# Loading the weights of Q, K and V with 32 instead of 4 rows outermost, in a two-layer graph attention kernel

## The chip, the cores and the metric

The kernel runs on one core of a Trainium2 chip. A core has five engines that run their own instruction queues in order and meet only at semaphores: TensorE (PE: matmuls, with weight loads as a second stream, PEld), VectorE (DVE), ScalarE (ACT), GpSimd (POOL) and SyncE (SP), which here only issues transfers. Sixteen DMA engines move data between HBM (the chip's memory) and SBUF (the core's working memory); TensorE writes its sums to PSUM. The metric is device time in microseconds (us), the median of several runs. All data are 32-bit floats.

## The reference

The input is a batch of 128 graphs of 128 nodes with 512 features, and one 128 x 128 adjacency matrix for each graph. Two layers follow each other, each with a residual and a layer norm:

```python
# layer 0
q, k, v = x @ Wq + bq, x @ Wk + bk, x @ Wv + bv        # 8 heads of 64
attn = softmax(where(adj > 0, q @ k.T / sqrt(64), -1e9))
x = layernorm(x + relu((attn @ v) @ Wo + bo))
# layer 1
Wh = x @ W
e = leaky_relu((Wh @ a1)[:, None] + (Wh @ a2)[None, :], 0.2)
x = layernorm(x + elu(softmax(where(adj == 0, -1e9, e)) @ Wh))
```

## The kernel before

The kernel works through 64 pairs of graphs. The five large products (Q, K, V, O and W) of a pair are done as block products in the manner of Strassen and Winograd: seven products (`PRODUCTS`) with sums of blocks on both sides, gathered in three PSUM banks A, B and C. The sums of the weight blocks are made once at the start (`weight_sums`, L131 to L134): for Q and K together they need both blocks of Wq and both of Wk. The sums on the left side (`left_sums`, L151 to L154, tiles sx, so, sz) are made for each pair, on GpSimd. VectorE and ScalarE empty the banks between the products (u2, u3, kT, qT, e1a, e1b and so on); a product that writes a bank again must wait for that.

Layer 1 doesn't multiply Wh by a1 and a2: `fold_a` (L203 to L213) multiplies W by a at the start (tiles wa_scr, wa_rep), `fold_t` and `fold_out` spread the result over the partitions (pwa, wa_bc), and `edge_term` (L490) then takes one product and sum for each graph. Each half of a is loaded by a transfer (a_bc) that GpSimd issues.

The attention weights are transposed in two steps: 32 x 32 blocks on VectorE (`weights_t`, prb), then out to HBM and back with the blocks reordered (`weights_out`, prd; `weights_in`, prT), from which `mix_values` (po) reads them. In layer 1 the row terms (pj), the edge matrix (pat) and the mixed nodes (pz) pass through TensorE.

The order of all this is not written as a loop. `at` gives every step of every pair a due time, PLAN[step] plus the pair's number times PERIOD, and the steps are recorded in the order of the due times. So PLAN sets only the order in which instructions stand in each engine's queue; their waits set the times. BUFS says how many buffers each kind of tile has: with one, a new tile waits until the last reader of the one before is done.

Ahead of the pairs come the loads of the weights, in this order: the first x blocks (xb), Wq, Wk, the adjacency matrix (adj), the second x blocks and adjacency matrix, then Wv, Wo and W. Wq and Wv are issued from ScalarE's queue, all else from SyncE's. Each load has one of eight completion semaphores and waits until the transfer that had it before is done. The rows of x are reordered in blocks of 32 (partition 32 v + r holds feature 128 v + r of a chunk), so Wq, Wk and Wv are loaded by `load_block_x` with the same order; Wo and W come row by row (`load_block`, L120).

The first work on VectorE waits for bq (bqs, L194), then scales both blocks of Wq (L196), transposes the first x blocks (L288) and makes the sums.

Of the kernel before, what the change touches and what calls it, by code (L numbers as in the profile page):

```python
# [14 lines left out]
N_BATCH = 128  # L15


PERIOD = 80.36
PLAN = dict(
    load_blocks=-203.35, load_adj=-141.65, x_transpose0=-108.79, x_transpose1=-80.72, sums_qk=-62.62, mask=-35.32,  # L20
    sums_v=-33.81, x_sums=-30.87, qk0=-30.03, qk_p1=-28.89, qk1=-24.47, qk_p1q=-23.84, qk_p6=-23.67, qk4=-22.15,
    qk3=-21.47, qk2=-20.46, qk_p7=-19.06, qk_c11=-17.42, qk_c22=-16.69, qk5=-15.77, v0=-13.29, sums_fold0=-12.95,
    v_p1=-11.35, fill_logits1=-10.97, qk6=-9.66, qk_c21=-9.52, v1=-8.33, v2=-7.72, v_p6=-6.99, v3=-6.55,
    fill_logits0=-4.19, qk_c12=-2.81, sums_o=-1.37, logits0=0.0, v_p7=1.78, mask_logits0=6.87, logits1=6.98,
    v4=8.58, v_c11=11.52, max_logits0=11.75, mask_logits1=12.17, v_c22=12.53, v5=17.32, max_logits1=17.42,
    v_c21=18.18, v6=18.57, v_c12=18.66, exp_logits0=26.37, sum_logits0=28.64, exp_logits1=31.22, norm_logits0=33.91,
    fill_edges0=36.7, sums_fold1=37.99, sums_fold_t0=42.14, sum_logits1=47.8, load_x0=56.09, norm_logits1=56.91,
    weights_t0=57.44, sums_fold_out0=60.06, weights_out0=61.6, weights_in0=62.47, sums_fold_t1=65.58,
    weights_t1=67.46, sums_fold_out1=74.55, mix_values0=81.46, weights_out1=82.7, weights_in1=84.68,
    mix_values1=87.22, mix_values_out0=94.58, mix_values_out1=96.97, sums_w=98.84, o_sums=103.62, o0=108.53,  # L30
    load_x1=109.41, o_p1=114.18, fill_edges1=114.73, o1=117.76, o_p1l=118.1, o2=120.61, o_p6=122.66, o3=122.75,
    o_p7=123.47, o4=123.68, o_c11=126.83, o_c22=129.32, o5=129.79, o_c21=130.83, residual01=132.36, o6=132.67,
    o_c12=133.46, stats01=133.46, mean01=133.56, residual00=134.07, rstd01=136.55, stats00=137.12, shift01=137.46,
    mean00=137.78, norm01=137.87, rstd00=137.95, edge_term01=138.68, edge_term11=139.19, shift00=140.27,
    norm00=141.75, edge_term10=142.12, edge_term00=142.31, edge_row1=143.18, edge_sums1=143.88, edge_row0=145.26,
    edge_leaky1=147.3, edge_sums0=147.37, edge_mask1=149.05, edge_leaky0=150.02, edge_max1=150.22,
    edge_mask0=151.47, edge_max0=152.05, edge_exp1=152.16, edge_exp0=152.23, edge_norm1=152.34, edges_t1=152.35,
    edges_t0=154.18, edges_t_out1=154.18, edge_norm0=154.29, mix_nodes1=154.39, edges_t_out0=154.42,
    mix_nodes0=154.6, mix_nodes_out1=156.09, mix_nodes_out0=157.89, z_sums=164.73, w0=173.41, w1=179.87,
    w_p1=181.52, w_p6=182.07, w2=182.1, w3=185.01, w_p7=187.54, w4=187.83, w_c11=188.88, w_c22=190.51, w5=195.11,  # L40
    w6=195.64, w_c21=198.1, elu_exp1=198.84, w_c12=200.38, elu_low1=215.59, elu_max1=222.2, elu_exp0=222.5,
    elu_low0=228.48, residual11=235.55, elu_max0=240.61, stats11=243.8, mean11=247.72, rstd11=249.46,
    residual10=251.29, shift11=265.27, stats10=269.96, mean10=297.04, finish1=299.37, rstd10=315.64, store1=320.24,
    shift10=323.36, finish0=332.2, store0=341.53)

ENDS = {}

BUFS = dict(
    xb=2, adj=4, xT=3, sx=2, pr=2, e1a512=1, e1b512=1, mask=1, u2512=1, u3512=2, qT=2, kT=2, e1a256=2, cv=2,
    u2256=1, u3256=1, t=2, scr=2, cw=4, prb=1, prT=2, oT=2, x=2, at=3, so=1, e1b256=2, co=5, e=2, attT=7, zT=2,  # L50
    sz=1)


# [1 line left out]
def tile_two_graph_layers(ctx: ExitStack, tc: tile.TileContext, x, adj, wq, bq, wk, bk, wv, bv, wo, bo, w, a, out,  # L55
# [9 lines left out]
    P = 128  # L65
    D = x.shape[2]
# [54 lines left out]

    def load_block_x(t, k, queue, src, rows, cols):

        for c in range(2):
            queue.dma_start(t[:, k, c, :], bass.AP(
                tensor=src.tensor, offset=src.offset + 32 * (2 * rows + c) * D + cols.start,
                ap=[[P * D, 4], [D, 32], [1, cols.stop - cols.start]]))

    def weight_sums(t, eng):
        b11, b21, b22, t1, t2, t3, t4 = (t[:, k, :, :] for k in range(7))  # L130
# [38 lines left out]
    wqk = block_weight("wqk", D)  # L169
    load_blocks(0)  # L170
    load_block_x(wqk, 0, nc.scalar, wq, 0, everything)
    load_block_x(wqk, 1, nc.scalar, wq, 1, everything)
    load_block_x(wqk, 5, nc.sync, wk, 0, everything)
    load_block_x(wqk, 2, nc.sync, wk, 1, everything)
    load_adj(0)
# [400 lines left out]
    def at(key, p, fn, *args):  # L576

        shift = ENDS.get(p if p < n_pair // 2 else p - n_pair, {}).get(key, 0.0)
        events.append((p * PERIOD + PLAN[key] + shift, len(events), fn, args))

# [69 lines left out]
```

## Time and profile before

Three runs took 2509.44, 2513.02 and 2514.66 us (median 2513.02). The profiled run had a span of 2509.6 us.

| Engine | busy us | share of the span |
|---|---|---|
| TensorE, matmuls | 2413.6 | 96% |
| TensorE, weight loads | 2190.1 | 87% |
| VectorE | 1912.0 | 76% |
| ScalarE | 1607.5 | 64% |
| GpSimd | 1459.9 | 58% |

The shares are means over the span. The matmuls of one pair follow each other in about 37.4 us, 64 pairs long, with a start and an end in which fewer steps overlap. The chain of work that ended last is 83% TensorE and 7% transfers. In the profile's lines, "L257" is the line of the kernel, "pBqk<-sx,wqk" the tile written and those read, "x16" the number of instructions in a row. Lines of waits give total time, number and the longest wait.

The loads of the weights in the profile are 4 transfers of 256 KB for Wq, 4 for Wk, and 8 of 128 KB for Wv, Wo and W each.

### The profile page before, as it was taken

The numbers are of one execution on the slowest core, as the hardware profiler recorded it, in microseconds if no ns is written. First come the engines' busy times: TensorE is split into PE (matmuls) and PEld (weight loads), VectorE is DVE, ScalarE is ACT, GpSimd is POOL, SyncE is SP. The second block draws the span as 40 slices with busy tenths as digits, with TensorE's granted clock in tenths as the row PEclk, the third lists the DMA queues.
The fourth block names the chain that finished last, engine by engine and source line by source line (L and its number), as shares of the span: only waits on it lengthen the run. The fifth ranks groups of instructions, "written<-read, shape, count | busy, mean of one in ns | idle before, by whom it ended". The sixth has DMA issues, their size and how long they took to land.

```text
span 2509.6 us, 51523 instructions
## 1 busy us (share of the span) xinstructions
PE 2413.6 (96%) x17928; PEld 2190.1 (87%) x17928; DVE 1912.0 (76%) x4031; ACT 1607.5 (64%) x5635; POOL 1459.9 (58%) x2053
## 2 busy tenths in 40 slices
PE   3999999999999999999999999999999999999995
PEld 3898998998998998998998898998988988989984
DVE  3777877877877877877877877877777877878775
ACT  0666666666666666676666666666666666666663
POOL 2356656656656656656656656556556556556554
PEclk8999999999999999999999999999999999999997
DMA  4323323423323323323423423323323323333222
GB/s 133 110 78 98 122 84 102 121 78 108 121 83 104 114 89 104 120 86 101 122 79 106 121 78 108 115 82 110 106 88 113 106 83 118 96 93 119 86 73 72
DMA packets 221076, 252.69 MB, mean 101 GB/s; under 512 B 19920, under 2 KB 170448, under 8 KB 220816
## 3 DMA queue, kind: packets, MB, share of 16 engines
q1 hardware_dynamic: 218896, 246.49, 32.3%
q8 instruction: 144, 2.36, 0.4%
q10 hardware_dynamic: 1584, 2.10, 0.2%
q14 instruction: 116, 0.95, 0.1%
q0 software_dynamic: 336, 0.79, 0.1%
HBM read 148.64 MB, written 100.66 MB: 99 GB/s over the span
## 4 chain that ended last, share of the span: by engine, by line
PE 83%; DMA 7%; DVE 6%; SPq 1%; ACT 1%; issue 1%; POOL 0%; ACTq 0%; POOLq 0%; DVEq 0%
PE pBqk L257 10%; PE pAqk L257 8%; PE pCqk L257 7%; PE pBw L246 7%; PE pBo L246 7%; PE pBv L246 6%; PE pCv L246 5%; PE s L403 5%; PE pAw L246 4%; PE pCw L246 4%; PE pAo L246 4%; PE pCo L246 4%; PE po L462 4%; PE pAv L246 3%; PE pz L538 3%; DMA prT<-prd 3%
## 5 line engine op out<-in xcount | busy, mean ns | idle before, releaser
L556 POOL TENSOR_SCALAR t<-t 128x512 f32<-128x512 f32 x126 | 255.0, 2024 | 414.7 <-ACT t L552 414.7
L426 ACT ACTIVATE pr<-pr,nmax 128x128 f32<-128x128 f32 x1024 | 396.0, 391 | 4.3 <-DVE nmax L420 4.3
L435 ACT ACTIVATE pr<-pr,tot 128x128 f32<-128x128 f32 x1024 | 313.8, 412 | 1.4 <-DVE tot L430 1.4
L257 PE MATMUL pBqk<-sx,wqk 128*128 128x128 f32 x2048 | 251.4, 276 | 22.3 <-DVE wqk L132 19.2
L257 PE MATMUL pAqk<-xT,wqk 128*128 128x128 f32 x2048 | 251.3, 276 | 19.1 <-DVE xT L288 19.1
L257 PEld LDWEIGHTS pBqk<-sx,wqk 128*128 128x128 f32 x2048 | 245.3, 193 | 26.1 <-issue 21.6
L273 POOL TENSOR_SCALAR rstd<-mv 128x1 f32<-128x1 f32 x256 | 81.3, 318 | 318.9 <-DVE mv L270 309.5
L257 PEld LDWEIGHTS pAqk<-xT,wqk 128*128 128x128 f32 x2048 | 245.4, 193 | 22.3 <-DVE xT L288 19.1
L415 DVE COPY_PREDICATED pr<-mask,s 128x1024 f32<-128x1024 int32 x128 | 173.5, 1355 | 112.0 <-PE s L403 112.0
L257 PE MATMUL pCqk<-sx,wqk 128*128 128x128 f32 x2048 | 250.0, 275 | 0.0
L257 PEld LDWEIGHTS pCqk<-sx,wqk 128*128 128x128 f32 x2048 | 244.6, 192 | 3.3
L301 ACT ACTIVATE e1aqk<-pAqk,bk 128x128 f32<-128x128 f32 x256 | 73.1, 368 | 246.1 <-PE pAqk L257 246.1
L426 ACT ACTIVATION_READ_ACCUMULATOR pr<-pr,nmax 128x1 f32 x1024 | 194.6, 190 | 0.0
L490 DVE SCALAR_TENSOR_TENSOR scr<-co,wa_bc 128x512 f32<-128x512 f32 x256 | 188.6, 773 | 1.9 <-ACT co L281 1.9
L274 POOL TENSOR_TENSOR rstd<-rstd,half 128x1 f32<-128x1 f32 x256 | 153.0, 597 | 21.3
L562 POOL TENSOR_TENSOR cw<-cw,co 128x512 f32<-128x512 f32 x126 | 160.0, 1270 | 0.0
L420 DVE TENSOR_REDUCE nmax<-pr 128x8 f32<-128x1024 f32 x128 | 155.7, 1216 | 2.2
L440 DVE STREAM_TRANSPOSE prb<-pr 128x1024 f32<-128x1024 f32 x128 | 156.4, 1222 | 0.6 <-DMA prd<-prb 0.6
L462 PE MATMUL po<-prT,cv 128*64 128x128 f32 x2048 | 134.4, 278 | 22.0 <-DMA prT<-prd 16.4
L278 POOL TENSOR_SCALAR nmean<-mv,rstd 128x1 f32<-128x1 f32 x256 | 135.4, 529 | 26.2
L471 ACT ACTIVATE oT<-po,bv 128x128 f32<-128x128 f32 x512 | 142.7, 383 | 12.1 <-PE po L462 11.5
L403 PE MATMUL s<-kT,qT 64*128 64x128 f32 x2048 | 148.7, 285 | 1.5 <-DVE pr L415 1.5
(150 smaller groups left out, 6155.3 us busy)
## 6 DMA issues: line engine op xcount, KB each, us to landing
prd<-prb SPq DMA_DIRECT2D x128, 512.0 KB
prT<-prd SPq DMA_DIRECT2D x512, 128.0 KB
xb<-in_x_dram SPq DMA_DIRECT2D x256, 128.0 KB
x<-in_x_dram SPq DMA_DIRECT2D x128, 256.0 KB
out_dram<-cw SPq DMA_DIRECT2D x128, 256.0 KB
adj<-in_adj_dram SPq DMA_DIRECT2D x64, 128.0 KB
wqk<-in_L_gnn_Wq_dram ACTq DMA_DIRECT2D x4, 256.0 KB
wv<-in_L_gnn_Wv_dram ACTq DMA_DIRECT2D x8, 128.0 KB
```

Source lines behind the costliest of these rows:

```text
L246: nc.tensor.matmul(out, left_block(left, blk.pair, a_i, c), weight[:, b_i, c, :], start=first and c == 0, stop=j in LAST and c == 1, skip_ ...
L257: nc.tensor.matmul(out[:, f * P:(f + 1) * P], weight[:, b_i, c, f * P:(f + 1) * P], left_block(left, blk.pair, a_i, c), start=first and f ...
L403: nc.tensor.matmul(ST["s", b][:, j, hp, :], q[r, hp, :], k[r, hp, :], start=True, stop=True)
L415: nc.vector.copy_predicated(PR[b], MASK[p][:, i, :].unsqueeze(1).to_broadcast([P, H, P]), ST.pop(("s", b)).rearrange("p j h k -> p (j h) k"))
L420: nc.vector.tensor_reduce(NMAX[b], PR[b], AX.X, ALU.max, negate=True)
L426: nc.scalar.activation(PR[b][:, h, :], PR[b][:, h, :], AF.Exp, bias=nmax[:, h:h + 1], scale=1.0, accum_out=TOT[b][:, h:h + 1])
L435: nc.scalar.activation(PR[b][:, h, :], PR[b][:, h, :], AF.Copy, scale=tot[:, h:h + 1])
L440: nc.vector.transpose(PRB[b].rearrange("p k h s -> p h k s"), PR.pop(b).rearrange("p h (k r) -> p h k r", r=32))
L462: nc.tensor.matmul(ST["o", b][j * DH:(j + 1) * DH, hp, :], v[:, h * DH:(h + 1) * DH], prT[:, :, j * (H // 2) + hp, :], start=True, stop=True)
L490: nc.vector.scalar_tensor_tensor(scr, X1[b], 1.0, wa_bc[s], op0=ALU.mult, op1=ALU.mult, accum_out=store[b])
L556: side_engine(b // 2).tensor_scalar(t, t, 1.0, -1.0, op0=ALU.min, op1=ALU.add)
L562: side_engine(b // 2).tensor_tensor(Y[b], Y[b], X1.pop(b), op=ALU.add)
```

## The change

`load_block_x` issued one transfer for each of the two chunks of 128 partitions of a block; the source of a transfer had three extents: 4 groups, 32 rows, the columns. Now it issues one transfer for each of the four groups of 32 partitions, with both chunks in it: 32 rows, 2 chunks, the columns. The same bytes land in the same places, in twice as many transfers of half the size. The aim is that the outermost extent of a transfer can be shared among more DMA engines.

With the load goes a new plan: other due times, another PERIOD and other buffer counts. The number and kind of the computing instructions stay the same; their order in the queues changes.

```diff
-PERIOD = 80.36
+PERIOD = 81.15
 PLAN = dict(
...
-    sums_v=-33.81, x_sums=-30.87, qk0=-30.03, qk_p1=-28.89, qk1=-24.47, qk_p1q=-23.84, qk_p6=-23.67, qk4=-22.15,
...
-    v_c21=18.18, v6=18.57, v_c12=18.66, exp_logits0=26.37, sum_logits0=28.64, exp_logits1=31.22, norm_logits0=33.91,
...
+    load_blocks=-235.76, x_transpose0=-108.28, x_transpose1=-83.64, sums_qk=-66.11, x_sums=-40.42, qk0=-37.67,
+    sums_v=-37.44, qk_p1=-36.74, qk1=-30.07, qk4=-29.33, load_adj=-28.84, qk_p6=-28.07, qk3=-26.31, qk_p1q=-23.26,
...
+    v6=16.67, max_logits1=18.8, v_c12=24.17, sums_o=26.55, exp_logits0=34.34, exp_logits1=36.2, sum_logits0=42.03,
+    fill_edges1=43.11, norm_logits0=45.17, sums_fold1=45.94, fill_edges0=53.74, sums_fold_t1=54.64,
...
 BUFS = dict(
-    xb=2, adj=4, xT=3, sx=2, pr=2, e1a512=1, e1b512=1, mask=1, u2512=1, u3512=2, qT=2, kT=2, e1a256=2, cv=2,
-    u2256=1, u3256=1, t=2, scr=2, cw=4, prb=1, prT=2, oT=2, x=2, at=3, so=1, e1b256=2, co=5, e=2, attT=7, zT=2,
+    xb=2, adj=4, xT=4, sx=2, pr=2, e1a512=1, e1b512=1, mask=2, u2512=1, u3512=1, qT=2, kT=2, e1a256=1, cv=2,
+    u2256=2, u3256=2, t=1, scr=1, cw=4, prb=2, prT=2, oT=3, x=2, at=4, so=1, e1b256=1, co=4, e=3, attT=2, zT=2,
     sz=1)
...
     def load_block_x(t, k, queue, src, rows, cols):
 
-        for c in range(2):
-            queue.dma_start(t[:, k, c, :], bass.AP(
-                tensor=src.tensor, offset=src.offset + 32 * (2 * rows + c) * D + cols.start,
-                ap=[[P * D, 4], [D, 32], [1, cols.stop - cols.start]]))
+        for q in range(4):
+            queue.dma_start(t[32 * q:32 * q + 32, k, :, :], bass.AP(
+                tensor=src.tensor, offset=src.offset + (q * P + 64 * rows) * D + cols.start,
+                ap=[[D, 32], [32 * D, 2], [1, cols.stop - cols.start]]))
```

More of the change, by code (lines that the diff above doesn't have):

```diff
@@ L15 @@
 N_BATCH = 128
-PERIOD = 80.36
+PERIOD = 81.15
 PLAN = dict(
-    load_blocks=-203.35, load_adj=-141.65, x_transpose0=-108.79, x_transpose1=-80.72, sums_qk=-62.62, mask=-35.32,
-    sums_v=-33.81, x_sums=-30.87, qk0=-30.03, qk_p1=-28.89, qk1=-24.47, qk_p1q=-23.84, qk_p6=-23.67, qk4=-22.15,
[L22 to L25, printed above, removed]
-    v_c21=18.18, v6=18.57, v_c12=18.66, exp_logits0=26.37, sum_logits0=28.64, exp_logits1=31.22, norm_logits0=33.91,
[L27 to L44, printed above, removed]
@@ new lines @@
+    load_blocks=-235.76, x_transpose0=-108.28, x_transpose1=-83.64, sums_qk=-66.11, x_sums=-40.42, qk0=-37.67,
+    sums_v=-37.44, qk_p1=-36.74, qk1=-30.07, qk4=-29.33, load_adj=-28.84, qk_p6=-28.07, qk3=-26.31, qk_p1q=-23.26,
+    qk_p7=-22.33, qk2=-21.08, qk5=-19.4, qk_c11=-19.04, qk_c22=-16.96, v0=-15.35, v_p1=-15.31, sums_fold0=-12.81,
+    qk_c21=-11.96, qk6=-11.86, v1=-11.78, mask=-11.73, v2=-10.23, fill_logits0=-5.35, v_p6=-4.04,
+    fill_logits1=-2.98, v3=-1.59, qk_c12=-1.49, logits0=0.0, sums_fold_t0=1.93, v_p7=6.47, mask_logits0=8.74,
@@ new lines @@
+    max_logits0=9.66, logits1=9.99, mask_logits1=11.82, v4=12.71, v_c11=13.04, v5=13.62, v_c22=15.62, v_c21=16.54,
+    v6=16.67, max_logits1=18.8, v_c12=24.17, sums_o=26.55, exp_logits0=34.34, exp_logits1=36.2, sum_logits0=42.03,
+    fill_edges1=43.11, norm_logits0=45.17, sums_fold1=45.94, fill_edges0=53.74, sums_fold_t1=54.64,
+    sum_logits1=54.86, weights_t0=55.3, weights_out0=58.66, norm_logits1=59.73, weights_in0=62.88, weights_t1=64.23,
+    load_x0=71.26, weights_out1=73.77, sums_fold_out1=73.84, weights_in1=78.83, sums_fold_out0=78.98,
@@ new lines @@
+    mix_values0=81.2, sums_w=83.22, mix_values1=87.74, load_x1=89.42, mix_values_out1=100.44,
+    mix_values_out0=100.75, o_sums=103.42, o0=111.81, o1=114.6, o_p1=116.39, o_p1l=116.55, o2=116.98, o_p6=117.15,
+    o3=119.0, o_c11=121.3, o_p7=121.45, o4=124.01, o_c22=124.02, o5=124.35, o_c21=124.42, o6=124.89,
+    residual01=125.47, stats01=125.52, o_c12=125.67, mean01=129.0, rstd01=130.22, residual00=130.71, stats00=131.64,
+    mean00=131.82, shift01=134.36, rstd00=135.95, norm01=136.02, shift00=137.89, edge_term01=138.98,
@@ new lines @@
+    edge_term11=139.63, norm00=141.64, edge_row1=143.56, edge_term10=144.69, edge_row0=144.74, edge_sums1=146.48,
+    edge_term00=148.15, edge_sums0=150.07, edge_leaky1=150.68, edge_mask1=152.18, edge_leaky0=152.53,
+    edge_max1=153.77, edge_mask0=154.04, edge_exp1=154.33, edges_t1=155.31, edge_max0=155.62, edge_exp0=155.97,
+    edges_t0=156.18, edges_t_out1=157.61, edges_t_out0=158.72, mix_nodes1=161.27, mix_nodes0=162.24,
+    edge_norm0=166.64, mix_nodes_out1=167.88, edge_norm1=169.48, mix_nodes_out0=175.44, w0=176.21, z_sums=179.2,
@@ new lines @@
+    w1=179.48, w_p1=181.69, w2=182.09, w_p6=182.38, w3=187.74, w4=191.97, w_p7=192.88, w_c11=192.91, w5=193.51,
+    w_c22=194.3, w_c21=194.82, w6=195.7, elu_exp1=196.91, w_c12=199.07, elu_low1=203.81, elu_max1=239.7,
+    residual11=244.56, stats11=246.99, elu_exp0=256.95, elu_low0=265.43, mean11=272.21, elu_max0=272.55,
+    rstd11=277.38, residual10=278.91, stats10=280.02, mean10=305.43, shift11=307.46, rstd10=308.49, finish1=324.38,
+    shift10=329.21, store1=336.09, finish0=338.18, store0=342.39)
```

## The prediction

> **What bounds the kernel now.** I read the shares of the engines first, then TensorE's waits over the whole run, then busy time by stretches, and last the first 70 us in order of time.
>
> ```profile
> PE 2413.6 (96%) x17928; PEld 2190.1 (87%) x17928; DVE 1912.0 (76%) x4031; ACT 1607.5 (64%) x5635; POOL 1459.9 (58%) x2053
> ...
> PE pBqk L257 <- DVE wqk L132: 19.2, 1, 19.2
> PE pAqk L257 <- DVE xT L288: 19.1, 1, 19.1
> PE po L462 <- DMA prT<-prd: 16.4, 22, 1.5
> PE pj L495 <- DVE scr L490: 13.3, 4, 5.5
> ```
>
> TensorE works 2413.6 of 2509.6 us; only the remaining 96 us can be won. Two single waits, each about 19 us long, make up 38 of them: the first product of Q and K waits for the transposed input, the second for the block sums of the weights (L132). The next wait, for the attention weights coming back from memory (prT), is spread over 22 places; the pj waits lie in the last 65 us.
>
> ```profile
> 0.00:20.00 20.00, 0.94 (x4) 0.95 (x5) 2.77 (x5) 0.00 (x0) 4.07 (x12) 1.00 0.35 107
> 20.00:42.00 22.00, 2.84 (x14) 2.54 (x12) 2.52 (x3) 3.46 (x9) 4.86 (x7) 0.64 0.41 131
> 42.00:70.00 28.00, 25.26 (x187) 23.52 (x188) 23.16 (x57) 7.91 (x37) 9.06 (x10) 0.91 0.50 136
> ...
> 1000.00:1400.00 400.00, 398.49 (x2987) 363.25 (x2985) 315.36 (x667) 264.60 (x922) 240.36 (x336) 1.00 0.34 103
> ```
>
> First the stretch, its length, then busy time of TensorE, weight loads, VectorE, ScalarE, GpSimd, the clock, the DMA share and rate. TensorE works under 4 us in the first 42; in the middle of the run it never rests. So the start is a stage bound by loads, and the other 2400 us are bound by TensorE.
>
> ```profile
> DVE wqk L131 <- DMA wqk<-in_L_gnn_Wk_dram: 13.2, 1, 13.2
> DVE wqk L132 <- DMA wqk<-in_L_gnn_Wk_dram: 6.7, 1, 6.7
> ...
> DMA packets 693, 0.98 MB, mean 98 GB/s; under 512 B 24, under 2 KB 376, under 8 KB 693
> q10 hardware_dynamic: 625, 0.94, 25.4%
> ...
> DMA packets 3131, 2.59 MB, mean 216 GB/s; under 512 B 295, under 2 KB 3053, under 8 KB 3131
> q1 hardware_dynamic: 3114, 2.58, 77.5%
> ```
>
> VectorE waits 19.9 us for W_K. The first pair of DMA lines is the stretch 10 to 20 us: Q and V weights, 98 GB/s, a steady quarter of the 16 engines. The second pair is 38 to 50 us, where W_O and W come through the row-wise load (L120): 2.59 MB. The first 2.25 us of that stretch still run at about 95 GB/s (0.22 MB), so the rest moved 2.37 MB in 9.75 us: 243 GB/s.
>
> **What the Trainium skill says.** "DMA: Bandwidth & Descriptors", section "Why a DMA increments its semaphore by 16 and not by 1": the number of engines is the largest one up to 16 that divides the slowest dimension of both sides. The old source starts with 4, the new one with 32: 4 engines, then 16. The quarter above agrees for 4; the new shape is not in this trace, though L96 loads 32 rows outermost too. Section "Issuing engines are not separate DMA queues" of the page: ScalarE's and SyncE's transfers share the same engines. The trace agrees: when W_K joins W_V after 23 us the rate stays near 98 GB/s. [...]prd needs 2.7 to 4.1 us from issue to the prT that waits for it. "TensorE: Matmul & The Clock Gate", "Part 1: The HAM clock gate": after idling TensorE starts at half rate. The first 16 matmuls take 3.78 us, later ones 1.95; both versions pay this, so I leave it out.
>
> **The change part by part.**
>
> *Loads.* 16 transfers on 4 engines become 32 on 16 engines; the bytes stay. Rate: at least 180 GB/s (smaller transfers, latency counted), at most 320 (the best slots of the 38 to 50 us stretch); I take 243. Bytes up to the end of W_K, from the sizes of the issues: xb 0.52, Q and K 2.10, bo 0.26, half of W_V interleaved 0.52, together 3.4 MB, 14.0 us; from the first bytes at 2 us this is 16 us. Up to the last byte of W (with W_V, W_O, W, two adj, the second xb, a): 7.08 MB, 29.1 us, so 31 us.
>
> *VectorE's chain, in the new order.* bq lands at 8.66 as before; then a scaling 0.69, two transposes 1.30, a scaling 0.69: 11.5. L131 runs before 16, L132 (1.23) from 16.1 to 17.3, and the second product starts near 17.5 instead of 42.08. L133 and L134 end at 19.7, the sums of W_V (2.8) at 22.5, u2qk (0.69) at 23.2; the third product starts at 23.3 instead of 49.31: 26 us earlier. SyncE's loads of the second xb and W_O come earlier with it.
>
> *What gives part of it back.* VectorE's queue then holds u3qk, kT (free at 26.6) and fold_a (L209, 3.4 us), which needs W, the last load:
>
> ```profile
> 52.70 0.41 DVE L209 SCALAR_TENSOR_TENSOR wa_scr<-w,a_bc 128x256 f32<-128x256 f32 x1
> ...
> 56.12 0.68 DVE L336 TENSOR_TENSOR qT<-pBqk,e1bqk 128x512 f32<-128x512 f32 x1
> ...
> 57.39 1.03 PE L246 MATMUL pBv<-wv,sx 128*128 128x256 f32 x4
> ```
>
> Before, W was there when fold_a's turn came. Now it isn't: fold_a waits from 26.6 to 31, ends at 34.5, qT (behind it, L336) at 35.2, and pBv, which needs the bank that qT empties, starts at 35.3 instead of 57.39: 22.1 us earlier. At 180 GB/s W lands at 41.3 and pBv starts at 45.5 (11.9 earlier); at 320 fold_a needn't wait, pBv starts at 30.8 (26.6 earlier).
>
> *Second pair.* With t=1 the second fold's a_bc1 can load only after the first fold; it is issued behind sx, 1.3 us late against fold 2 (landing takes 5.0 to 6.2 us). ScalarE now does e1aqk ahead of norm_logits (2.34 us), which removes the 1.9 us that pBqk waited for u2qk at 74.47. Net 1.3 earlier.
>
> *New due times, other buffer counts: the steady part.* Each engine has the same instructions. I walked one pair (37.4 us) through the new order with the durations of 1238 to 1277 us. TensorE's closest place is pCo, which needs the bank that the move of pCw (L394) empties, and L394 now stands behind bn_stats (L267): counted from the start of pBo, u2o begins at 1.06, takes 0.34 of the queue, L267 0.58, L394 itself 0.42, which is 2.40, and 0.14 for the semaphore (wqk's end at 41.94 to pBqk at 42.08) makes 2.54; pCo's turn comes three products of 0.864 later, at 2.59: 0.05 us of slack. The others: second s after mask_logits 0.24; pat after exp 0.4 (both pj now stand together); Av after qT 0.6. None is negative. t=1 (exp, min, max of one tile end before the next starts), scr=1, u3512=1, attT=2, e1a256=1 and co=4 all come out free, co with 2.4 us. po: prb of the second matrix is ready about 0.8 us earlier in the period, po's turn 0.1 us earlier, but a load of x (256 KB) stands just ahead of the store prd. I count no change of the 17 us that po waits in 400 to 2400 us. Edge rows, mask, fills and end lie beside TensorE's work or move by under 0.5 us in the last 65 us: nothing.
>
> Sum: 22.1 + 1.3 = 23.4 us less than 2513: **2490**.
>
> **The rivals.**
> - *The new order costs a wait per pair.* 0.05 us of slack is less than the spread of a single instruction, and prd may queue behind x. 0.4 us in each of 64 pairs is 26 us, which eats the gain: 2516, slower than before. For it: VectorE is 76% busy, and single VectorE instructions stretch (L490 1.09 instead of 0.68) when GpSimd runs. Against: the walk finds no negative slack.
> - *Less gain, as the loads stay serial.* Eight semaphores, 2 to 3 us each, and W at 40 us: 2503. For it: more, smaller transfers (W_V 64 KB). Against: W_O's 128 KB transfers reached 243 GB/s under the same semaphores.
> - *More gain.* prb's 0.8 us clear most of po's 17 us: 2513 - 23 - 15 = 2475. Against: x ahead of prd.
>
> **How the numbers follow.** Forecast 0.62, wait per pair 0.15, less gain 0.13, more gain 0.10. The range has to reach the less-gain case with some of the rest and most of the more-gain case: 2474 to 2509. Slower by over 5 us needs the wait per pair at 0.45 us or more: 0.10. Within 5 us: 0.07. Faster: 0.83.
>
> **What would show it.** Right: between 10 and 20 us the DMA share is well over a half; L132 ends near 17 us; VectorE waits some 4 us for W at L209; pBv near 35 us; TensorE without rest from 1000 to 1400. Wrong: W later than 40 us, bq late and bqs holding VectorE, or TensorE waits at pCo, pat, s or po in every pair.

## The result, and the profile after

The changed kernel took 2523.63 us (median of four runs, 2520.54 to 2525.28); the kernel before, run beside it on the same chip, 2513.84 us. The ratio is 1.004, with a 95% interval of 1.0022 to 1.0057: slower, by about 10 us. 2490 us was forecast.

The start went as meant. By stretches (start and length, then busy time of TensorE, weight loads, VectorE, ScalarE and GpSimd, the clock, the DMA share and rate), the kernel after shows this:

```profile
0.00:20.00 20.00, 3.78 (x16) 3.49 (x16) 6.29 (x7) 0.00 (x0) 8.95 (x18) 1.00 1.00 200
20.00:42.00 22.00, 18.42 (x112) 16.98 (x112) 16.26 (x34) 5.34 (x15) 6.75 (x7) 0.94 0.68 172
1000.00:1400.00 400.00, 389.82 (x2916) 356.52 (x2915) 303.57 (x652) 261.02 (x918) 224.53 (x333) 1.00 0.34 101
```

In the first 20 us the DMA share is 1.00 where it was 0.35, the rate 200 GB/s where it was 107. TensorE is busy 18.42 us between 20 and 42 where it was 2.84. But the last line has a change, too: in the middle of the run TensorE now rests 10.2 us in 400, where it rested 1.5. TensorE's shares and its waits over the whole run:

```profile
PE 2416.2 (96%) x17928; PEld 2201.7 (87%) x17928; DVE 1884.8 (75%) x4031; ACT 1601.8 (64%) x5635; POOL 1403.6 (56%) x2053
```

```profile
PE po L462 <- DMA prT<-prd: 34.3, 29, 2.8
PE po L462 <- ACT zT L543: 11.9, 12, 1.1
PE pAqk L257 <- DVE xT L288: 9.8, 1, 9.8
PE pj L495 <- DVE scr L490: 8.0, 3, 5.6
PE pBqk L257 <- DVE wqk L132: 7.0, 1, 7.0
...
PE po L462 <- ACT t L552: 4.9, 3, 1.7
```

The two waits of 19 us at the start are now 9.8 and 7.0. At the top stands po. The profile puts its waits down to three causes, but zT and t are never read by po, so I count all three as waits for prT: 51 us. Before, po's waits are 22 us together (prT 16.4, cv 4.9, and 0.5 "issue", for which the profile shows no cause). po's wait has become the largest of the run.

Where in the run the time goes is seen from when pz starts in each pair (the first pz of the pair, from the trace in order of time):

| | pz of the first pair | first to last pz | last pz to the end | span |
|---|---|---|---|---|
| before | 115.96 | 2370.0 | 23.6 | 2509.6 |
| after | 99.21 | 2395.6 | 24.0 | 2518.8 |
| difference | -16.8 | +25.6 | +0.4 | +9.2 |

So the loads brought 16.8 us by the first pair's pz, and 63 pairs lost 0.41 us each. Between the tenth and the sixtieth pz a pair takes 37.82 us before and 38.26 after. Of these 0.44 us, waits shown ahead of TensorE's instructions are 0.43 (0.34 before, 0.77 after). The remainder is two terms that nearly cancel, taken from start to start of TensorE's groups with the shown waits subtracted. The groups around the waiting po (s, po, pCv) take 0.17 us more, of which 0.12 are four places where the clock fell to one half after a wait (the last section shows one). The groups around the pat transposes (pCqk, pat, pBv), which now stand together, take 0.16 less.

SyncE's queue shows what po waits for. A step "prd" is the store of the attention weights, "prT" the load that reads them back; prT's first issue waits until prd has landed. First the kernel before, then the kernel after, in order of time (start, length):

```profile
1241.13 0.38 SPq L571 DMA_DIRECT2D out_dram<-cw  x1
1242.64 0.34 SPq L446 DMA_DIRECT2D prd<-prb  x1
1245.38 1.90 SPq L453 DMA_DIRECT2D prT<-prd  x4
```

```profile
1235.14 0.33 SPq L446 DMA_DIRECT2D prd<-prb  x1
1237.82 1.75 SPq L453 DMA_DIRECT2D prT<-prd  x4
1239.91 0.35 SPq L105 DMA_DIRECT2D x<-in_x_dram  x1
1240.49 0.34 SPq L446 DMA_DIRECT2D prd<-prb  x1
1244.47 1.74 SPq L453 DMA_DIRECT2D prT<-prd  x4
```

and TensorE in the kernel after, at the po that reads this second prT:

```profile
1247.99 1.09 PE L462 MATMUL po<-prT,cv 128*64 128x128 f32 x16
1250.19 1.09 PE L462 MATMUL po<-prT,cv 128*64 128x128 f32 x16 [1.10 <-DMA prT<-prd]
```

The first prd of the pair, with nothing close ahead, is read back 2.68 us after its issue. The second, 0.58 us behind a load of x (0.9 in the median), 3.98 us after; in the kernel before the second took 2.74, although a store of a result (256 KB, out_dram) had been issued 1.5 us ahead of it. Over all pairs the median from issue to read-back of the second prd is 3.09 us before and 4.01 after; that of the first is 2.7 in both. prT waits for prd itself and for no other transfer: in the kernel after it is issued 0.05 us (median) after prd has landed.

### The profile page after: what moved, and what is told of

The parts are those of the page before. It is cut to its first block, busy times and chain, and to the rows that moved or that the text cites. A ratio compares the mean times of both kernels' runs of the same rounds, so it can differ in the third digit from the quotient of the medians.

```text
span 2518.8 us, 51745 instructions
## 1 busy us (share of the span) xinstructions
PE 2416.2 (96%) x17928; PEld 2201.7 (87%) x17928; DVE 1884.8 (75%) x4031; ACT 1601.8 (64%) x5635; POOL 1403.6 (56%) x2053
## 4 chain that ended last, share of the span: by engine, by line
PE 80%; DMA 8%; ACT 6%; DVE 3%; SPq 2%; issue 1%; POOL 0%; POOLq 0%; DVEq 0%
PE pBqk L257 10%; PE pAqk L257 8%; PE pBw L246 7%; PE pCqk L257 7%; PE pBo L246 7%; PE pBv L246 5%; PE pCv L246 5%; PE pAw L246 4%; PE s L403 4%; PE pAo L246 4%; PE pCw L246 4%; PE po L462 4%; DMA prT<-prd 4%; PE pCo L246 4%; PE pAv L246 3%; DMA prd<-prb 3%
## 5 line engine op out<-in xcount | busy, mean ns | idle before, releaser
L273 POOL TENSOR_SCALAR rstd<-mv 128x1 f32<-128x1 f32 x256 | 104.8, 409 | 423.3 <-DVE mv L270 412.5
L556 POOL TENSOR_SCALAR t<-t 128x512 f32<-128x512 f32 x126 | 245.8, 1951 | 14.4 <-ACT t L552 9.4
L490 DVE SCALAR_TENSOR_TENSOR scr<-co,wa_bc 128x512 f32<-128x512 f32 x256 | 171.8, 671 | 59.8 <-ACT co L281 57.5
L411 POOL MEMSET pr<- 128x1024 f32 x128 | 121.8, 952 | 122.2 <-DVE prb L440 122.2
L462 PEld LDWEIGHTS po<-prT,cv 128*64 128x64 f32 x2048 | 112.3, 138 | 70.3 <-ACT zT L543 19.9
L274 POOL TENSOR_TENSOR rstd<-rstd,half 128x1 f32<-128x1 f32 x256 | 146.5, 572 | 21.3
```

What stands on the lines that cost most here:

```text
L274: nc.gpsimd.tensor_tensor(RSTD[key], RSTD[key], half, op=ALU.pow)
L462: nc.tensor.matmul(ST["o", b][j * DH:(j + 1) * DH, hp, :], v[:, h * DH:(h + 1) * DH], prT[:, :, j * (H // 2) + hp, :], start=True, stop=True)
L490: nc.vector.scalar_tensor_tensor(scr, X1[b], 1.0, wa_bc[s], op0=ALU.mult, op1=ALU.mult, accum_out=store[b])
L556: side_engine(b // 2).tensor_scalar(t, t, 1.0, -1.0, op0=ALU.min, op1=ALU.add)
```

## The experiments

Theory 1: the load of x (256 KB) just ahead of the second prd delays its completion, and with it prT and po, in nearly every pair. Theory 2: prb or po have moved in the new order, and x has no part. Theory 3: what is issued behind prT slows prT's own landing. "Waits in a pair" below are those that TensorE shows between the tenth and the sixtieth pz, divided by 50; "read-back" is the median from the issue of the second prd to that of its prT. Each ratio is to the kernel before on the same chip; on the chip of most of these runs that kernel took some 2505 us, 8 to 10 less than above.

### x behind the second prT

```diff
-    load_x0=71.26, weights_out1=73.77, sums_fold_out1=73.84, weights_in1=78.83, ...
+    load_x0=79.0, weights_out1=73.77, sums_fold_out1=73.84, weights_in1=78.83, ...
```

> The kernel after, with one due time changed: the first matrix's x (256 KB, load_x0) is issued behind the second matrix's prT instead of just ahead of its prd. Theory 1 (the x load just ahead of prd delays prd's completion, so prT and po, in nearly every pair): the second prd needs about 2.7 us to prT's issue instead of 4 to 5, TensorE's waits for prT fall from some 50 us to 20 or less, and the time is 2490 to 2500 us. Theory 2 (prd and prT are late because the new order makes prb late or po early, x has no part in it): waits stay near 50 us and the time is 2515 to 2528 us. Theory 3 (what follows prT, the loads of xb and x, slows prT's landing): x now follows prT too, so waits of 50 us or more, 2523 us or more.

Measured: 2462.67 us, ratio 0.9829 (0.9816 to 0.9843). One due time turns the slowdown into a gain of 43 us. TensorE's waits in this kernel, largest first:

```profile
PE pAqk L257 <- DVE xT L288: 10.0, 1, 10.0
PE pj L495 <- DVE scr L490: 8.0, 3, 5.6
PE pBqk L257 <- DVE wqk L132: 7.2, 1, 7.2
PE po L462 <- DMA prT<-prd: 6.2, 12, 1.5
```

and SyncE's queue:

```profile
1248.98 0.34 SPq L446 DMA_DIRECT2D prd<-prb  x1
1253.19 1.73 SPq L453 DMA_DIRECT2D prT<-prd  x4
1254.97 0.43 SPq L105 DMA_DIRECT2D x<-in_x_dram  x1
```

po's waits fall from 51 to 7 us. The median read-back is 3.12 us; this one still took 4.2, and 27 of the 64 took over 3.4, about as many as in the kernel before (26). What delays those is not shown. Theory 2 falls, since prb and po have kept their places; theory 3 falls, since x now follows prT and does no harm. The time is 27 us under the lower end of what theory 1 had said, and 8 of the 27 are the chip. I had compared with the kernel before, whose own po waits and order also left something: a pair takes 37.39 us here, 0.43 under the kernel before, of which 0.24 is less waiting and the rest the shorter groups at pat and po.

### The loads alone, and the plan alone

The kernel before with the new `load_block_x` and nothing else; and the kernel after with the old one:

```diff
-                ap=[[P * D, 4], [D, 32], [1, cols.stop - cols.start]]))
+                ap=[[D, 32], [32 * D, 2], [1, cols.stop - cols.start]]))
```

> The kernel before with the new load_block_x alone; due times, period and buffer counts are the old ones. All theories say that the loads themselves gain at the start and touch nothing later: the first product of pair 1 some 15 to 20 us earlier than before (67.06 us), po's waits near 22 us as before, time 2493 to 2499 us. A rival in which smaller transfers cost something in the steady part, or in which the old order gains less at the start: 2503 us or more.

Measured: 2483.78 us, ratio 0.9917 (0.9904 to 0.993). A second run of the same kernel:

> The loads alone once more, beside the kernel with the transposes together on the same chip: ratio 0.990 to 0.993.

Measured, on another chip: 2492.10 us, ratio 0.9927 (0.9915 to 0.994). So the loads alone are worth 19 to 22 us. The first pair's pz starts 18.6 and 19.9 us earlier than before. The two profiles differ in the steady part: po's waits are 0.19 us in a pair in one and 0.38 in the other, and first to last pz 2367.4 and 2375.4 us. A program's waits at po thus vary by some 8 us from one profile to another, which bounds what a single trace can tell here.

> The kernel after with the old load_block_x (4 rows outermost); new due times, period and buffer counts stay. If the loss is in the new order's steady part, po's waits stay near 50 us, and the start is as slow as before or slower: 2538 to 2548 us. If the loss came from the new transfers themselves (their shape, their number), the time is near before, 2510 to 2518 us.

Measured: 2524.01 us, ratio 1.007 (1.0056 to 1.0084). The plan and buffers without the loads cost 18 us; its pair takes 38.17 us, with 0.72 us of waits. So the loss is in the plan. But I had expected at least 14 us more: the loads under the new plan change the ratio by only 0.003, although pz of the first pair starts 18.9 us earlier with them. The traces put the remainder in the steady part: first to last pz takes 2386.4 us here and 2395.6 in the kernel after, with the same instructions. That is 9 us, about what two profiles of one program differed by above; why the waits are longer in one than in the other is not settled.

### x ahead of the second prd in the kernel before

```diff
-    ... sum_logits1=47.8, load_x0=56.09, norm_logits1=56.91,
+    ... sum_logits1=47.8, load_x0=82.6, norm_logits1=56.91,
```

> The kernel before with one due time changed: the first matrix's x is issued just ahead of the second matrix's prd instead of ahead of the first's. Theory 1: the second prd needs 4 to 5 us to prT's issue instead of 2.7 to 4.1, po's waits rise from some 22 us to 45 or more, time 2530 to 2545 us. Theory 2: no change, 2511 to 2517 us.

Measured: 2572.29 us, ratio 1.027 (1.0256 to 1.0284). Old loads, old buffers, old order but for this load, and the loss appears, larger than expected. SyncE's queue in this kernel shows what may make it larger:

```profile
1269.35 0.36 SPq L571 DMA_DIRECT2D out_dram<-cw  x1
1269.76 0.42 SPq L105 DMA_DIRECT2D x<-in_x_dram  x1
1270.58 0.32 SPq L446 DMA_DIRECT2D prd<-prb  x1
1274.53 1.74 SPq L453 DMA_DIRECT2D prT<-prd  x4
```

The store of a result (256 KB) stands ahead of prd here, too, 1.2 us, so that up to 512 KB are ahead. The median read-back is 4.34 us, waits 1.15 us in a pair (0.34 before). The same store stood there in the kernel before, which read back after 3.09, so it is x that makes the difference; what the store adds to it was not tried by itself.

### How many bytes ahead

In the kernel after, x in two halves of 64 rows, one ahead of prd and one behind prT; and both x loads of the pair ahead of prd:

```diff
-        nc.sync.dma_start(X[b], x[b])
+        nc.sync.dma_start(X[b][0:64], x[b][0:64])
...
+        nc.sync.dma_start(X[b][64:P], x[b][64:P])
...
+    load_x0=71.26, load_x_rest0=79.0, weights_out1=73.77, ...
```

> The kernel after, with the first matrix's x loaded in two transfers of 64 rows (128 KB each): one stays just ahead of the second prd, the other is issued behind the second prT. If prd is delayed by the bytes that stand ahead of it, half the bytes cost half the delay: the waits for prT lie midway between 7 us (x behind) and 51 us (x ahead), some 25 to 30 us, and the ratio to before is near 0.993 (midway between 0.983 and 1.004). If a transfer as such delays it, whatever its size: as the kernel after, ratio 1.00 to 1.006.

```diff
-    mix_values0=81.2, sums_w=83.22, mix_values1=87.74, load_x1=89.42, ...
+    mix_values0=81.2, sums_w=83.22, mix_values1=87.74, load_x1=71.27, ...
```

> The kernel after, with both x loads of a pair (512 KB) just ahead of the second prd. If the bytes ahead delay it, the delay doubles: prd needs 5.5 to 7 us to prT's issue, and as the wait at po is then over a microsecond in every pair, waits of 120 us or more; ratio 1.03 to 1.045. If a transfer as such delays it, or the delay came from somewhere else: ratio 1.00 to 1.01.

| just ahead of the second prd | read-back, us | waits in a pair, us | a pair, us | ratio |
|---|---|---|---|---|
| no x (x behind) | 3.12 | 0.10 | 37.39 | 0.9829 |
| 128 KB | 3.42 | 0.32 | 37.65 | 0.9913 (0.9899 to 0.9927) |
| 256 KB (the change) | 4.01 | 0.77 | 38.26 | 1.004 |
| 512 KB | 4.53 | 1.38 | 39.13 | 1.0285 (1.0266 to 1.0304) |

In all four rows the last transfer of the first prT stands 1.4 to 1.5 us ahead as well. The loss grows with the bytes: half an x costs 0.3 us of read-back and a ratio slightly better than midway, so it isn't the transfer as such. po's waits with half an x are 22 us (19.6 for prT, 2.1 "issue"), where 25 to 30 were expected. With 512 KB the direction is as expected, the size less: read-back 4.53 us, not 5.5 to 7. po's waits

```profile
PE po L467 <- DMA prT<-prd: 19.6, 29, 2.1
```

with half an x (whose lines count five more than the others'), and with two

```profile
PE po L462 <- DMA prT<-prd: 67.2, 47, 3.4
PE po L462 <- ACT t L552: 11.3, 7, 1.9
...
PE po L462 <- ACT cw L281: 4.5, 2, 2.3
...
PE po L462 <- ACT zT L543: 3.5, 3, 1.3
PE po L462 <- issue: 3.0, 5, 0.8
```

90 us together, not the 120 or more that I had set. The first of the two x is issued 1.0 us ahead of prd there (median), so part of it may have moved by then.

The Trainium skill offers a mechanism, in "DMA: Bandwidth & Descriptors", section "Queues, rings and completion order": each DMA engine takes descriptors in the order of its ring, and the increment of a transfer's semaphore lands only after every earlier write from that engine. So a store's completion waits for the bytes of the load ahead of it. The table agrees with that: 128, 256 and 512 KB ahead add 0.30, 0.89 and 1.41 us. It doesn't part this from prd's own bytes moving later behind those of x; either way the bytes ahead are what is paid.

### x ahead of the first prd

```diff
-    load_x0=71.26,
+    load_x0=57.0,
```

> The kernel after, with the first matrix's x issued ahead of the first prd instead of ahead of the second. The first prT has some 5 us to spare before its po's turn, so a delay of about 2 us there is hidden: theory 1 says waits for prT near 7 us and a ratio of 0.981 to 0.987, as with x behind. If any x load among these stores costs the same: 1.00 or more.

Measured: 2466.81 us, ratio 0.9857 (0.9843 to 0.987). SyncE's queue:

```profile
1239.89 0.34 SPq L105 DMA_DIRECT2D x<-in_x_dram  x1
1245.88 0.33 SPq L446 DMA_DIRECT2D prd<-prb  x1
1248.54 1.75 SPq L453 DMA_DIRECT2D prT<-prd  x4
```

The forecast time came, but not by the reason given for it: x is issued 6 us ahead of the first prd, has landed long before, and prd isn't delayed at all (2.66 us). "Ahead of" in the order is not what counts; x cost at about a microsecond and not at 6 us. That is also why the kernel before, which has x in this place, didn't suffer.

For what lies between, the kernel before has distances of its own, those of the result's store to the second prd. At its nearest:

```profile
2077.39 0.38 SPq L571 DMA_DIRECT2D out_dram<-cw  x1
2077.87 0.38 SPq L446 DMA_DIRECT2D prd<-prb  x1
2081.60 1.74 SPq L453 DMA_DIRECT2D prT<-prd  x4
```

Four pairs have it 0.47 us ahead and read back after 3.7 to 4.0 us, four 0.9 ahead and take 3.3, two 1.2 ahead and take 3.0 to 3.1; most have it 1.5 ahead and take 2.7 at the least (though a third of these take about 4, as said above). So this delay shrinks with the distance and is gone at 1.5 us. The last transfer of the first prT is 0.5 us further ahead in each of these pairs, and the traces don't part the two. x at 0.9 us cost more than this store did; no run shows whether that is because it is a load.

### The fold behind qT

```diff
-    sums_fold0=-12.81,
+    sums_fold0=-11.5,
```

with x behind the second prT as above.

> The kernel after with x behind the second prT, and the first fold of a (L209) placed behind the qT that frees the bank of the V products. It takes away the 1.3 us that these waited for qT, once; nothing in the steady part: ratio 0.981 to 0.984, at best 1 to 2 us under the kernel with x behind alone.

Measured: 2461.63 us, ratio 0.9837 (0.9823 to 0.9851). The wait of pBv for qT is gone, and one of the same 1.3 us for u2v, behind the fold on VectorE, takes its place. No gain that these runs can tell from the kernel with x behind alone.

### The transposes together

The loads alone, and the pj and pat transposes of a pair each moved next to each other:

```diff
-edge_row1=143.18, edge_sums1=143.88, edges_t1=152.35
+edge_row1=145.2, edge_sums1=145.9, edges_t1=154.175
```

> The kernel before with the new loads, and in addition the two pj transposes of a pair placed next to each other and the two pat transposes likewise (the order that the changed kernel has); due times otherwise the old ones. If the TensorE time that the new order saves (0.16 us in a pair by the starts of its instructions) comes from these transposes, the products around them take 0.1 to 0.16 us less in a pair: 6 to 10 us under the loads alone, ratio 0.987 to 0.990, unless the first pat, now later, makes others wait. If it comes from somewhere else in the order: as the loads alone, 0.991 to 0.993.

Measured: 2526.00 us, ratio 1.0059 (1.0045 to 1.0072). Slower, for another reason; TensorE's waits:

```profile
PE pBv L246 <- DVE qT L336: 23.1, 63, 0.9
PE pz L538 <- ACT attT L531: 15.2, 62, 0.2
...
PE po L462 <- DMA prT<-prd: 1.4, 2, 1.1
```

The move brought two waits into every pair, 38 us together, and TensorE, later now, finds prT ready. So this run doesn't say what the transposes are worth; the 0.16 us in a pair stays a reading of the traces.

## Why the prediction was wrong

**The failed step is the one on po.** It reads: "a load of x (256 KB) stands just ahead of the store prd. I count no change of the 17 us that po waits in 400 to 2400 us." These 17 us became 40 (prT 24.5, zT 10.9, t 4.9), while with x behind they were 5. The step saw both sides. One was right: prb leaves earlier against po's turn. prd's issue at 1240.49 is 8.6 us ahead of po's turn (1250.19 less the wait of 1.10), and 7.9 before (1242.64 to the second 16 of po, about 1250.6; the last section has the line): 0.7 us gained. But the other side, x, was given no price, and the two were set equal. The read-back grew by 0.92 us in the median, 1.24 in the pair shown. An estimate was at hand from the prediction's own rates: 256 KB at 180 to 243 GB/s are 1.1 to 1.5 us, against 0.7 gained, on a path where TensorE already waited in 30 places. That is 0.4 us or more in a pair, and 0.41 was lost. That the two agree so well is in part luck: the read-back grew by less than estimated, and the loss also holds the half clock.

**The half clock** was left out of the prediction, as both kernels pay it at the start. The kernel after pays it four times more, behind waits of po of 1.7 to 2.8 us: 6 us in the run. The kernel before has no wait at po of 1.6 us or more, and pays none there.

**The rival that came true** is the wait per pair, given 0.15: 26 us in 64 pairs, 2516. It was right in size, and the start, which brought 16.8 us and not 23.4, makes up most of what is missing to 2523.63. Of its two reasons, prd behind x was the one; pCo's slack of 0.05 us held, as no wait at pCo shows.

**The start**: right in kind, short in size. 22.1 us at pBv and 1.3 in the second pair were forecast. VectorE's chain in the kernel after:

```profile
13.90 2.38 DVE L196 TENSOR_SCALAR wqk<-wqk 128x1024 f32<-128x1024 f32 x1 [3.53 <-DMA wqk<-in_L_gnn_Wq_dram]
16.21 1.20 DVE L131 TENSOR_TENSOR wqk<-wqk 128x1024 f32<-128x1024 f32 x1
19.29 1.23 DVE L132 TENSOR_TENSOR wqk<-wqk 128x1024 f32<-128x1024 f32 x1 [1.88 <-DMA wqk<-in_L_gnn_Wk_dram]
...
30.99 1.48 DVE L209 SCALAR_TENSOR_TENSOR wa_scr<-w,a_bc 128x256 f32<-128x256 f32 x1
```

That 32 rows outermost use all the engines held: the share went from 0.35 to 1.00. But W_K was there at 19.3 us, not 16, for two reasons. The rate was 220 GB/s from 2 us on, not 243 (both inside the bounds of 180 and 320), and 3.8 MB moved in that time, not the 3.4 counted: the 256 KB of a, landed at 17.5 us, were not in that sum. The second product started at 20.66 and not 17.5. The fold of a began at 30.99 without a wait for W: that wait, forecast as 4 us, didn't come, because the queue itself was 4 us late. Its first two steps took 1.48 and 1.37 us instead of 0.42, beside GpSimd's sums of W_O, which ended at 33.6. pBv started at 38.00, 19.4 us earlier, not 22.1:

```profile
38.00 1.13 PE L246 MATMUL pBv<-wv,sx 128*128 128x256 f32 x4 [2.15 <-DVE qT L336]
```

Of these, 16.8 are left at pz of the first pair, after a wait of 2.8 us of po at 71 us, already the second prd behind x.

**The steady part besides po**: the walk found no negative slack at pCo, s, pat and Av, and no new waits stand there. The smaller buffer counts did no harm: the kernel with x behind has them all, and 0.10 us of waits in a pair. What the walk didn't see is that the new order saves 0.16 us of TensorE at the pat transposes, some 10 us in the run. **The end**: nothing was forecast, 0.4 us came.

**Less gain** and **more gain** were wrong in the sum. But the second, 2475, was near what the change had in it: with x moved, 2462.67, and as the ratio of 0.9829 was measured on a faster chip, an estimated 2471 on this one.

## What to carry to other kernels

When a plan moves a transfer, price it against the next completion that somebody waits for: its bytes by the measured rate, if it is issued within about a microsecond ahead, and nothing if it is some microseconds ahead. How fast the price falls between may stand in the traces already, in pairs or iterations where the distance differs by chance. Set that against the slack of the waiting engine; a place that already waits in the profile has none, and each pair or iteration pays. When two effects pull against each other, give each a number before calling them even; and when a gain at the start doesn't show in the total, look at a stretch in the middle first.

## What the hardware did that was not expected

A wait of TensorE costs more than its idle time, by two steps. The first is small and comes with every wait. In the kernel before the stream runs on through 32 matmuls of po:

```profile
1249.64 1.97 PE L462 MATMUL po<-prT,cv 128*64 128x128 f32 x32
1251.53 0.38 PE L403 MATMUL s<-kT,qT 64*128 64x128 f32 x2
```

They take 1.89 us from their start to that of s. (The profile models the ends of matmuls, so starts are what to go by.) In the pair of the kernel after that is shown above, the same 32 take 3.22 (1247.99 to 1251.21, where s starts), of which 1.10 is the wait: 2.12, or 0.2 us more.

The second step comes behind some of the longer waits. In the kernel after, TensorE in order of time, and a stretch of it with the clock (columns as above, the clock 0.50):

```profile
2283.97 1.09 PE L462 MATMUL po<-prT,cv 128*64 128x128 f32 x16 [2.20 <-DMA prT<-prd]
2284.99 1.88 PE L403 MATMUL s<-kT,qT 64*128 64x128 f32 x16
2286.80 2.03 PE L246 MATMUL pCv<-wv,sx 128*128 128x256 f32 x4
2288.66 1.03 PE L246 MATMUL pBv<-wv,xT 128*128 128x256 f32 x4
```

```profile
2285.30:2288.60 3.30, 3.30 (x20) 2.79 (x17) 1.35 (x1) 0.94 (x4) 2.23 (x2) 0.50 0.82 267
```

The clock is one half for over 3 us. From the end of the wait to pBv these three groups take 4.7 us; behind most waits they take 3.1. Over the twelve traces, the last pairs left out, this followed 21 of the 43 waits of po of 1.74 us or more, and none of the 332 shorter ones; what decides among the longer ones is not shown. The kernel after has it four times (1.4 to 1.6 us each), the one with two x ahead twelve times, the kernels before and with x behind not at all behind po. So the groups s, po and pCv, shown waits subtracted, take 6.01 us in a pair with x behind (waits 0.10), 6.21 in the kernel after (0.77) and 6.46 with two x ahead (1.38).
